# Opening of a fused transformer block on one core: where the first weight product's operands are loaded and cast, and in which order its last quarter and the first transposes run

## The chip, the cores and the metric

The kernel runs on one core of a Trainium2 chip. The metric is the device time of one execution in microseconds (us); the kernel before has a median of 939.83 us over three runs (939.63 to 941.84). The core has a matrix engine (TensorE, PE in the profile; its weight loads are listed apart as PEld), VectorE (DVE), ScalarE (ACT), GpSimd (POOL), and SyncE (SP), which in this kernel mostly issues transfers. Operands lie in SBUF, matrix results in PSUM; the inputs come by DMA.

## The reference, cut to what matters

Four blocks follow one another on a (2, 1024, 512) activation, each with a layer norm ahead of it and a residual around it:

```python
x = x + attn_a(layernorm(x), Wq, bq, Wk, bk, Wv, bv, Wbeta, ...)   # chunked linear attention, 4 heads of 128, chunks of 128
x = x + ffn(layernorm(x), wq_gate, s_gate, wq_up, s_up, wq_down, s_down)
x = x + attn_b(layernorm(x), W_q, W_k, W_v, W_o)                   # softmax attention over 1024 tokens, width 512
x = x + ffn(layernorm(x), ...)                                     # the same weights again

def layernorm(x): return (x - mean(x)) / sqrt(var(x) + 1e-5)

# attn_b
Q, K, V = x @ W_q, x @ W_k, x @ W_v
scores = (Q @ K.T) / sqrt(512)
out = softmax(scores) @ V @ W_o

# attn_a, its projections
q = x @ Wq + bq;  k = x @ Wk + bk;  v = x @ Wv + bv
```

Since `scores` is `x @ (W_q @ W_k.T) @ x.T`, the kernel computes the 512 x 512 matrix M = W_q W_k^T once, at the very beginning, and spills it for the third block. M does not depend on the activations, so it can run while the first activations are loaded and normalized. All large products are computed from pairs of numbers: a value is rounded to the matrix engine's fast 32-bit format (the high part), and what is lost is kept as a second number in the same format (the low part). A product of two such pairs is three matmuls: high x high, high x low, low x high.

## The kernel before, in words

Activations are worked on in tiles of 128 tokens x 512 features (16 tiles, NT), four tiles to a group. The code is written as a list of operations in program order; a planner decides from its own estimate of the times in which order each engine runs its own instructions, and adds the semaphores. Two helpers steer it: `behind(inss)` (line 61) makes every instruction that is written inside it come after the given instructions on the same engine's queue (it adds no wait across engines), and the tile pools fix how many buffers of a kind exist.

The opening, up to about 25 us:

- Line 347: `ones`, 128 x 128, filled by GpSimd. Lines 663 to 665: `WARM` = 8 matmuls of `ones` with `ones` in plain 32-bit format into a scratch bank (16 instructions in the trace, two to a matmul).
- `split` (line 68) is a cast by ScalarE into the high part and a subtraction for the low part, by VectorE unless another engine is given. `load_split` (line 73) is a transfer of 256 KB on SyncE's queue into a staging tile, and a `split` of it; the low part's instruction is kept in the list `parts`.
- `product_operands` (line 143) loads for each of four 128-row slices k of the contraction the left operand (W_q transposed) and the right operand (W_k transposed) with `load_split`. For M the low part of the right operand is computed by GpSimd (line 148). The first two slices use the four `stg` buffers, the last two a room that later takes Wq.
- Lines 676 to 680: the eight transfers for M, then four tiles of x, then the small gate weights. `split_M` is the last two low parts (the left one by VectorE, the right one by GpSimd).
- `weight_product` (line 152) is a generator. For each k it issues 12 matmuls (four output blocks of 128 rows, `mm3` each) and yields. Matmuls of one k can be ordered by the planner as it likes, except that each output bank accumulates.
- Lines 682 to 686: after k = 2 the tiles 0 and 1 are normalized and transposed by the matrix engine (four transposes a tile), the last slice k = 3 is put behind those transposes, and tiles 2 and 3 follow it.
- `layernorm` (line 100): statistics on VectorE (`bn_stats`, `bn_aggr`, `ve` = variance + eps), the power -1/2 on GpSimd (`rs`), then the normalized tile `xn` on VectorE. With `chained` a tile's `bn_stats` goes behind the `ve` of the tile before. `layernorm_T` (line 115) adds the four transposes and the split of their result into `xh` (ScalarE) and `xl` (VectorE).
- Line 687: Wk is loaded and split, its VectorE instructions behind the last `xn` and behind `split_M`. Then come the constants, Wq (staged in the room of M's operands), the first Wk product (`pWk`), the gate projection (`pab`, which reads `xh` and `xl` of all four tiles) and the Wq products (`pq`).

Of the kernel before, what the change touches and what calls it, by code (L numbers as in the profile page):

```python
# [9 lines left out]
F32 = mybir.dt.float32  # L10
# [3 lines left out]
ALU = mybir.AluOpType  # L14
AX = mybir.AxisListType

P = 128
D = 512
KD = D // P
# [8 lines left out]
NC = T // P  # L28
EPS = 1e-5
ZERO_POINT = 128.0  # L30
WARM = 8


@with_exitstack
def hybrid_block_kernel(ctx: ExitStack, tc: tile.TileContext, a, out):
    nc = tc.nc

    cp = ctx.enter_context(tc.tile_pool(name="const", bufs=1))
# [8 lines left out]
    def psum(name):  # L47
        return pp.tile([P, 512], F32, tag="ps", name=name)

    def slot(name, dt=F32R):  # L50

        return wp.tile([P, 2048], dt, tag="slot", name=name)


    ident = cp.tile([P, P], F32, name="ident")
    make_identity(nc, ident)
    mhalf = cp.tile([P, 1], F32, name="mhalf")
# [3 lines left out]
    def behind(inss):  # L61

        es = ExitStack()
        for ins in inss:
            es.enter_context(tc.issue_after(ins))
        return es

    def split(hi, lo, src, eng=None):

        c = nc.scalar.copy(hi, src)  # L70
        return c.ins, (eng or nc.vector).tensor_tensor(lo, src, hi.bitcast(F32), ALU.subtract).ins  # L71

    def load_split(w, sp, src_ap, name, eng=None, stg=None):

        if stg is None:
            stg = sp.tile([P, 512], F32, tag="stg", name=f"stg_{name}")
        load = nc.sync.dma_start(out=stg, in_=src_ap).ins
        cast, low = split(w[:, 0:512], w[:, 512:1024], stg, eng)
        parts.append(low)
        return cast, load  # L80


    def mm3(ps, lhs_hi, lhs_lo, rhs_hi, rhs_lo, first, last):
        nc.tensor.matmul(ps, lhs_hi, rhs_hi, start=first, stop=False)  # L84
        nc.tensor.matmul(ps, lhs_hi, rhs_lo, start=False, stop=False)  # L85
        end = nc.tensor.matmul(ps, lhs_lo, rhs_hi, start=False, stop=last).ins  # L86
        ends[id(ps)] = end
        return end

    ends, normed_x, parts, copied, varied = {}, [], [], [], []  # L90

    def new_xT(name):
        return tuple(slot(f"{n}_{name}").rearrange("p (k c) -> p k c", k=KD) for n in ("xh", "xl"))

    def load_x(src, name, tag="xin"):
        xin = (rp if tag == "xres" else xp).tile([P, D], F32, tag=tag, name=f"xin_{name}")
        nc.sync.dma_start(out=xin, in_=src)
        return xin

    def layernorm(xin, name, chained=False):  # L100

        bn = mp.tile([P, 6], F32, tag="bn", name=f"bn_{name}")
        with behind(varied if chained else ()):
            nc.vector.bn_stats(bn, xin)
        mv = mp.tile([P, 2], F32, tag="mv", name=f"mv_{name}")
        nc.vector.bn_aggr(mv, bn)
        ve = mp.tile([P, 1], F32, tag="ve", name=f"ve_{name}")
        varied[:] = [nc.vector.tensor_scalar(ve, mv[:, 1:2], EPS, None, ALU.add).ins]  # L108
        rs = mp.tile([P, 1], F32, tag="rs", name=f"rs_{name}")
        nc.gpsimd.tensor_tensor(rs, ve, mhalf, ALU.pow)  # L110
        xn = xp.tile([P, D], F32, tag="xn", name=f"xn_{name}")
        normed_x[:] = [nc.vector.tensor_scalar(xn, xin, mv[:, 0:1], rs, ALU.subtract, ALU.mult).ins]
        return xn

    def layernorm_T(xin, xT, i, name):

        xn = layernorm(xin, name, True)
        ps = psum(f"pxT_{name}").rearrange("p (k c) -> p k c", k=KD)
        for k in range(KD):
            turned = nc.tensor.transpose(ps[:, k, :], xn[:, k * P : (k + 1) * P], ident).ins  # L120
        xh, xl = xT
        cs = bass.ts(i, P)
        split(xh[:, :, cs], xl[:, :, cs], ps)
        return turned
# [18 lines left out]
    def product_operands(sp, lhsT_d, rhs_d, name, k, rooms=(None, None)):  # L143

        w = slot(f"{name}{k}")
        lw, rw = w[:, 0:1024], w[:, 1024:2048]
        load_split(lw, sp, lhsT_d[k * P : (k + 1) * P, :], f"{name}l{k}", None, rooms[0])
        eng = nc.gpsimd if name == "M" else None
        cast, _ = load_split(rw, sp, rhs_d[k * P : (k + 1) * P, :], f"{name}r{k}", eng, rooms[1])
        return lw, rw, cast  # L150

    def weight_product(operands, name):

        ps = [psum(f"p{name}{m}") for m in range(KD)]
        for k in range(KD):
            lw, rw, _ = operands[k]
            for m in range(KD):
                end = mm3(
                    ps[m],
                    lw[:, m * P : (m + 1) * P],  # L160
                    lw[:, 512 + m * P : 512 + (m + 1) * P],
                    rw[:, 0:512],
                    rw[:, 512:1024],
                    k == 0,
                    k == KD - 1,
                )
            yield ps, end

    def spill(pool, tags, ps, dst, name):
# [10 lines left out]
    def ln_norm(src, nm, st, i):  # L180


        t = st * ST + i
        for n in range(t, min(t + 2, st * ST + ST)):
            if (nm, n) not in lnX:
                lnX[nm, n] = load_x(src[n], f"{nm}{n}")
        if i == 0:
            lnY[nm, st] = yp.tile([P, 4, KD, ST, 32], F32, tag="y", name=f"y_{nm}{st}")
        xn = layernorm(lnX[nm, t], f"{nm}{t}")
        done = nc.vector.transpose(lnY[nm, st][:, :, :, i, :], xn.rearrange("p (k b q) -> p b k q", k=KD, b=4))  # L190
        laid[:] = [done.ins]
# [149 lines left out]
    with ExitStack() as actx:  # L341
        ap = actx.enter_context(tc.tile_pool(name="attn_a", bufs=2))
        a1 = actx.enter_context(tc.tile_pool(name="attn_a1", bufs=1))
        a3 = actx.enter_context(tc.tile_pool(name="attn_a3", bufs=3))
        sp = actx.enter_context(tc.tile_pool(name="stage", bufs=4))

        ones = a1.tile([P, P], F32, name="ones")
        nc.gpsimd.memset(ones, 1.0)

        le = a1.tile([P, P], F32, name="le")  # L350
        nc.gpsimd.affine_select(
            out=le, in_=ones, compare_op=ALU.is_ge, fill=0.0, base=0, pattern=[[1, P]], channel_multiplier=-1
# [11 lines left out]
        xTa, aba, gta, sca, qTa, kva, ata, deca, sta, rowa, facta = ({} for _ in range(11))  # L364
# [31 lines left out]
        xa = [x_in[t * P : (t + 1) * P, :] for t in range(NT)]  # L396

        def ln_tile(t):
            st, i = divmod(t, ST)
            if i == 0:  # L400
                xTa[st] = new_xT(f"a{st}")
            tag = "xres" if t < 8 and t % 4 > 1 else "xin"
            return layernorm_T(xs[t] if t < 4 else load_x(xa[t], f"a{t}", tag), xTa[st], i, f"a{t}")

        def gate_proj(st):

# [256 lines left out]
        pw = psum("warm")  # L663
        for i in range(WARM):
            nc.tensor.matmul(pw[:, 0:P], ones, ones, start=i == 0, stop=i == WARM - 1)
        loads, xs = [], []
        prep = weight_product(loads, "M")

        def staging(name):
# [5 lines left out]
        for k in range(KD):  # L675
            rooms = (room[:, 2 * k - 4], room[:, 2 * k - 3]) if k > 1 else (None, None)
            loads.append(product_operands(sp, a["WqT"], a["WkT"], "M", k, rooms))
        xs += [load_x(xa[t], f"a{t}", "xres" if t > 1 else "xin") for t in range(ST)]
        load_wab()
        split_M = parts[-2:]  # L680
        turned = []
        for k in range(KD):
            with behind(turned):
                pm, end = next(prep)
            with behind((end,)):
                turned = [ln_tile(t) for t in ((), (), (0, 1), (2, 3))[k]]
        with behind((*normed_x, *split_M)):
            load_wqkv("Wk")
        load_consts()
# [6 lines left out]
        for i in range(4):  # L696
            ends.clear()
            q_head(0, i)
            with behind((wq_loaded, *ends.values())):
                for t in ((), (4,), (5,), (6, 7))[i]:  # L700
                    ln_tile(t)
            if i == 1:
                with behind((*normed_x, *copied)):
                    spill(ap, ("kT", "kw", "sdec", "at"), pm, m_d, "M")
# [22 lines left out]
        for t in range(NT):  # L727
# [13 lines left out]
            if t == NT - 2:  # L741
                with behind(key_copy):
                    for n in (1, 2):
                        loads.append(product_operands(sp, a["WvT"], a["Wo"], "V", n))
                with behind(parts[-4:]):
                    late_norm.pop()()
# [28 lines left out]
            if t == NT - 2:  # L775
                prep = weight_product(loads, "V")
# [541 lines left out]
```

## Time and profile before

| what | value |
|---|---|
| median of three runs | 939.83 us (939.63 to 941.84) |
| the profiled execution, its own time | 939.53 us |
| its span, from the first to the last instruction | 937.8 us |
| TensorE busy | 931.0 us, 99% of the span |
| VectorE, ScalarE, GpSimd busy | 723.2, 411.1, 218.6 us |
| mean granted TensorE clock | 1.000 |
| first matmul of M starts | 4.93 us |
| first matmul of the first Wk product starts | 18.95 us |

In a line of the timeline the columns are: start in us from the first instruction, duration in us, engine, line of the code, operation, output and inputs by the program's names, sizes, and how many instructions were merged into the line; in brackets the idle time of the engine ahead of it and what ended that. For merged lines the duration is from the first start to the last end. In the table by stretch the columns are the length, and for each engine the busy time with the number of instructions, then the granted clock, the share of the time in which the DMA engines were busy, and their rate. `pM` is M in PSUM, `stg_Ml` and `stg_Mr` are the staged left and right operands of the first two slices, `y_M` those of the last two, `pxT_a` is a transposed tile.

### The profile page before, as it was taken

To read this page: it belongs to the slowest core of one execution; us is meant where nothing else is said; L and a number is where in the kernel's file an instruction comes from. 1 tells how busy PE (TensorE), PEld (TensorE's weight loads), DVE (VectorE), ACT (ScalarE), POOL (GpSimd) and SP (SyncE) were. 2 spreads that over 40 slices of the span, in tenths; PEclk is the share of its full clock that TensorE was granted. 3 is DMA by queue.
4 is the path that set the end of the run, shared out by engine and by line. 5 is a ranking of instruction groups with operands and counts; after the bars stand their busy time and mean duration, and the time that the engine had idled before them with its cause. 6 is when DMAs were issued, how large, how long until landed. Compare 5 with 4: busy or idle time off the path is not lost.

```text
span 937.8 us, 13217 instructions
## 1 busy us (share of the span) xinstructions
PE 931.0 (99%) x4402; PEld 773.1 (82%) x4402; DVE 723.2 (77%) x1461; ACT 411.1 (44%) x795; POOL 218.6 (23%) x320
## 2 busy tenths in 40 slices
PE   9999999999999999999999999999999999999998
PEld 7788888888778888888888888888878888888887
DVE  7867767779989799787947878658978876976655
ACT  5653434335665444444324535235434444434421
POOL 3233323444655001120120400031400531001100
PEclk9999999999999999999999999999999999999999
DMA  9536456585699566734852989326979852663012
GB/s 326 181 101 173 143 118 185 184 210 199 251 342 305 148 218 213 162 92 117 281 125 57 170 170 238 108 36 130 200 152 366 260 154 46 242 212 124 34 66 82
DMA packets 215605, 162.18 MB, mean 173 GB/s; under 512 B 150960, under 2 KB 166640, under 8 KB 215536
## 3 DMA queue, kind: packets, MB, share of 16 engines
q1 hardware_dynamic: 212624, 153.72, 56.4%
q0 software_dynamic: 2912, 7.61, 4.2%
q8 instruction: 35, 0.57, 0.3%
q14 instruction: 34, 0.28, 0.1%
HBM read 104.76 MB, written 41.84 MB: 156 GB/s over the span
## 4 chain that ended last, share of the span: by engine, by line
PE 94%; DMA 3%; DVE 1%; SPq 1%; issue 0%; ACT 0%; DVEq 0%; ACTq 0%
PE pog L901 4%; PE pog L900 4%; PE pof L901 4%; PE pof L900 4%; PE pVg L331 4%; PE pZg L331 4%; PE pXg L331 4%; PE pVf L331 4%; PE pZf L331 4%; PE pXf L331 4%; PE pob L86 3%; PE pob L84 3%; PE pob L85 3%; PE pYg L331 2%; PE pYf L331 2%; PE psV L1000 2%
## 5 line engine op out<-in xcount | busy, mean ns | idle before, releaser
L900 PE MATMUL pog<-wdg,hsg 128*128 128x512 f32 (+1 forms) x165 | 60.1, 375 | 0.0
L901 PE MATMUL pog<-wdg,hsg 128*128 128x512 f32 (+1 forms) x165 | 60.1, 375 | 0.0
L901 PE MATMUL pof<-wdf,hsf 128*128 128x512 f32 x154 | 59.2, 390 | 0.0
L900 PE MATMUL pof<-wdf,hsf 128*128 128x512 f32 x154 | 59.2, 389 | 0.0
L84 PE MATMUL pob<-vh,pth 128*128 128x512 f32 x128 | 50.1, 392 | 0.4 <-ACT pth L70 0.4
L86 PE MATMUL pob<-vh,ptl 128*128 128x512 f32 x128 | 50.2, 392 | 0.0
L85 PE MATMUL pob<-vl,pth 128*128 128x512 f32 x128 | 49.9, 390 | 0.0
L331 PE MATMUL pVf<-T_f,wcf 128*128 128x512 f32 x176 | 46.8, 390 | 0.0
L331 PE MATMUL pXg<-B_g,wcg 128*128 128x512 f32 x176 | 46.7, 389 | 0.0
L331 PE MATMUL pVg<-T_g,wcg 128*128 128x512 f32 x176 | 46.4, 389 | 0.0
L331 PE MATMUL pXf<-B_f,wcf 128*128 128x512 f32 x176 | 46.4, 392 | 0.0
L71 POOL TENSOR_TENSOR hsg<-sgg,hsg 128x128 fp32r<-128x128 f32 x40 | 18.0, 469 | 114.8 <-ACT hsg L70 78.8
L110 POOL TENSOR_TENSOR rs_g<-ve_g,mhalf 128x1 f32<-128x1 f32 x16 | 9.6, 604 | 134.3 <-DVE ve_g L108 134.3
L201 POOL DMA_DIRECT2D xT_g<-y_g x48 | 30.9, 651 | 40.6 <-DVE T_b L71 30.1
L331 PEld LDWEIGHTS pXf<-B_f,wcf 128*128 128x128 f32 x176 | 32.7, 188 | 7.7 <-issue 0.7
L110 POOL TENSOR_TENSOR rs_b<-ve_b,mhalf 128x1 f32<-128x1 f32 x16 | 10.4, 655 | 121.6 <-DVE ve_b L108 121.6
L331 PEld LDWEIGHTS pVf<-T_f,wcf 128*128 128x128 f32 x176 | 33.0, 188 | 7.0
L331 PEld LDWEIGHTS pXg<-B_g,wcg 128*128 128x128 f32 x176 | 33.1, 188 | 6.9
L331 PEld LDWEIGHTS pVg<-T_g,wcg 128*128 128x128 f32 x176 | 33.1, 188 | 6.9
L900 PEld LDWEIGHTS pog<-wdg,hsg 128*128 128x128 f32 x165 | 31.1, 188 | 5.7
L901 PEld LDWEIGHTS pog<-wdg,hsg 128*128 128x128 f32 x165 | 31.0, 188 | 5.6
L900 PEld LDWEIGHTS pof<-wdf,hsf 128*128 128x128 f32 x154 | 28.9, 188 | 6.0
(340 smaller groups left out, 2735.7 us busy)
## 6 DMA issues: line engine op xcount, KB each, us to landing
wcg<-wc SPq DMA_DIRECT2D x21, 896.0 KB, 5.2
wc<-wcf SPq DMA_DIRECT2D x11, 896.0 KB, 6.5
wcf<-wc SPq DMA_DIRECT2D x10, 896.0 KB, 6.6
p<-py SPq DMA_DIRECT2D x15, 512.0 KB, 3.9
ptl<-p SPq DMA_DIRECT2D x56, 128.0 KB, 3.9
xin_a<-in_x SPq DMA_DIRECT2D x16, 256.0 KB, 4.9
xra<-in_x SPq DMA_DIRECT2D x16, 256.0 KB, 3.0
row<-cl SPq DMA_DIRECT2D x16, 256.0 KB, 4.0
```

The costliest lines, as they stand in the source:

```text
L71: return c.ins, (eng or nc.vector).tensor_tensor(lo, src, hi.bitcast(F32), ALU.subtract).ins
L84: nc.tensor.matmul(ps, lhs_hi, rhs_hi, start=first, stop=False)
L85: nc.tensor.matmul(ps, lhs_hi, rhs_lo, start=False, stop=False)
L86: end = nc.tensor.matmul(ps, lhs_lo, rhs_hi, start=False, stop=last).ins
L110: nc.gpsimd.tensor_tensor(rs, ve, mhalf, ALU.pow)
L201: (nc.sync if sync else nc.gpsimd).dma_start(out=xf[32 * b : 32 * (b + 1), :, c, :], in_=y[32 * c : 32 * (c + 1), b].rearrange("p k i q -> ...
L331: nc.tensor.matmul(ps, w[:, m, k * P : (k + 1) * P], o[:, s, k, :], start=first and k == 0 and s == 0, stop=k == 1 and s == 1, skip_group_ ...
L900: nc.tensor.matmul(ps, hs[i][0][:, j], wd[j][:, ds], start=j == 0, stop=False)
L901: nc.tensor.matmul(ps, hs[i][1][:, j], wd[j][:, ds], start=False, stop=j == KH - 1)
L1000: ends[nm] = nc.tensor.matmul(ps, o[:, i, k], w[:, j, k], start=first and k == 0 and i + j == 0, stop=k == 1 and i == 1, skip_group_check= ...
```

## The change

Five edits, all in the opening:

1. `ones` is filled by VectorE, ahead of everything else in the program, and the warm-up has 6 matmuls in place of 8.
2. For M's first slice the right operand's transfer is issued on ScalarE's queue, the left one's on SyncE's as before. The right operand is cast by VectorE, the left one by ScalarE; the left low part is VectorE's, behind that cast; the right low part stays with GpSimd.
3. For the other three slices the low part of the right operand is computed by VectorE, and the casts and subtractions of M are put one behind the other in the order left, right, left, right.
4. The statistics of tiles 0 and 1 are issued on their own, behind M's last two low parts; `layernorm` takes them as known.
5. M's last slice is cut in two: output blocks 0 and 1 precede the transposes of tiles 0 and 1, blocks 2 and 3 follow them, then come tiles 2 and 3.

```diff
-WARM = 8
+WARM = 6
...
+    ones = cp.tile([P, P], F32, name="ones")
+    nc.vector.memset(ones, 1.0)
     ident = cp.tile([P, P], F32, name="ident")
...
-    def layernorm(xin, name, chained=False):
-
+    def statistics(xin, name, chained):
         bn = mp.tile([P, 6], F32, tag="bn", name=f"bn_{name}")
...
         nc.gpsimd.tensor_tensor(rs, ve, mhalf, ALU.pow)
+        return mv, rs
+
+    def layernorm(xin, name, chained=False, known=None):
+
+        mv, rs = known or statistics(xin, name, chained)
         xn = xp.tile([P, D], F32, tag="xn", name=f"xn_{name}")
...
-        load_split(lw, sp, lhsT_d[k * P : (k + 1) * P, :], f"{name}l{k}", None, rooms[0])
-        eng = nc.gpsimd if name == "M" else None
-        cast, _ = load_split(rw, sp, rhs_d[k * P : (k + 1) * P, :], f"{name}r{k}", eng, rooms[1])
+
+        first = name == "M" and k == 0
+        if first:
+            stg = [sp.tile([P, 512], F32, tag="stg", name=f"stg_M{n}0") for n in "lr"]
+            nc.scalar.dma_start(out=stg[1], in_=rhs_d[0:P, :])
+            nc.sync.dma_start(out=stg[0], in_=lhsT_d[0:P, :])
+            cast = nc.vector.tensor_copy(rw[:, 0:512], stg[1])
+            with behind((cast.ins,)):
+                casts[:] = split(lw[:, 0:512], lw[:, 512:1024], stg[0])
+            nc.gpsimd.tensor_tensor(rw[:, 512:1024], stg[1], rw[:, 0:512].bitcast(F32), ALU.subtract)
+            return lw, rw, cast.ins
+        queue_up = name == "M"
+        with behind((*parts[-1:], *casts) if queue_up else ()):
+            casts[:] = [load_split(lw, sp, lhsT_d[k * P : (k + 1) * P, :], f"{name}l{k}", None, rooms[0])[0]]
+        with behind((*parts[-1:], *casts) if queue_up else ()):
+            cast, _ = load_split(rw, sp, rhs_d[k * P : (k + 1) * P, :], f"{name}r{k}", None, rooms[1])
+            casts[:] = [cast]
         return lw, rw, cast
...
                     k == KD - 1,
                 )
+                if m == 1 and name == "M" and k == KD - 1:
+                    yield ps, end
             yield ps, end
...
-        ones = a1.tile([P, P], F32, name="ones")
-        nc.gpsimd.memset(ones, 1.0)
...
-        for k in range(KD):
+        known = {}
+        for k in range(KD + 1):
             with behind(turned):
                 pm, end = next(prep)
-            with behind((end,)):
-                turned = [ln_tile(t) for t in ((), (), (0, 1), (2, 3))[k]]
+            if k == 0:
+                with behind(split_M):
+                    for t in (0, 1):
+                        known[t] = statistics(xs[t], f"a{t}", True)
+            with behind((end, *varied)):
+                turned = [ln_tile(t) for t in ((), (), (), (0, 1), (2, 3))[k]]
```

## The prediction

> **What bounds the kernel now.** I read the engine totals first, then the waits of TensorE, then the opening in order of time, then the busy time by stretch. The totals:
>
> ```profile
> span 937.8 us, 13217 instructions
> ...
> PE 931.0 (99%) x4402; PEld 773.1 (82%) x4402; DVE 723.2 (77%) x1461; ACT 411.1 (44%) x795; POOL 218.6 (23%) x320
> ```
>
> TensorE is idle for 937.8 - 931.0 = 6.8 us in all. No edit shortens a product, so only idle time, the warm-up and slow spacing of matmuls can be won. TensorE's waits over the whole span:
>
> ```profile
> PE warm L665 <- POOL ones L348: 1.3, 1, 1.3
> PE pxT_a L120 <- DVE xn_a L112: 0.6, 1, 0.6
> PE pYf L331 <- DVE haf L828: 0.5, 1, 0.5
> PE pob L84 <- ACT pth L70: 0.4, 1, 0.4
> ```
>
> Two of the four lie in the opening, and the change aims at both. The opening in order of time:
>
> ```profile
> 1.27 3.78 PE L665 MATMUL warm<-ones 128*128 128x128 f32 x16 [1.27 <-POOL ones L348]
> ...
> 3.54 0.62 ACT L70 CAST M<-stg_Ml 128x512 fp32r<-128x512 f32 x1 [1.46 <-DMA stg_Ml<-in_WqT]
> ...
> 4.20 0.69 DVE L71 TENSOR_TENSOR M<-stg_Ml,M 128x512 fp32r<-128x512 f32 x1 [1.99 <-ACT M L70]
> 4.26 0.62 ACT L70 CAST M<-stg_Mr 128x512 fp32r<-128x512 f32 x1
> ...
> 4.93 1.38 PE L84 MATMUL pM<-M 128*128 128x512 f32 x4
> 4.96 1.29 POOL L71 TENSOR_TENSOR M<-stg_Mr,M 128x512 fp32r<-128x512 f32 x1 [3.16 <-ACT M L70]
> ...
> 6.30 0.50 PE L85 MATMUL pM<-M 128*128 128x512 f32 x1
> ...
> 8.10 2.94 DVE L71 TENSOR_TENSOR M<-y_M,M 128x512 fp32r<-128x512 f32 x2 [0.81 <-ACT M L70]
> ...
> 8.81 3.38 POOL L71 TENSOR_TENSOR M<-y_M,M 128x512 fp32r<-128x512 f32 x2
> ...
> 10.96 0.68 DVE L104 BATCH_NORM_STATS2 bn_a<-xin_a 128x6 f32<-128x512 f32 x1
> ...
> 14.89 0.66 PE L120 MATMUL pxT_a<-ident,xn_a 128*128 128x128 f32 x4 [0.60 <-DVE xn_a L112]
> ...
> 22.52 0.43 PE L411 MATMUL pab<-xl_a,wab 128*48 128x512 f32 x1
> ```
>
> Full-width matmuls follow each other by 0.227 us when nothing holds them (the four merged in 1.07 us at 8.25: three spacings and one length of 0.39). Against that, four losses are seen. The product begins at 4.93. Its first slice takes 8.25 - 4.93 = 3.32 us where 12 x 0.227 = 2.72 are needed: 0.60 lost, to slow first matmuls and to GpSimd's low part, which ends at 6.25 with L85 at 6.30. Tile 1's transposes start 0.87 after the last one of tile 0 where 0.11 is the step: 0.76 lost. And at 22.52 the gate projection starts 0.49 after the matmul before it: 0.26 lost, waiting for xl of tile 3 from VectorE. The table by stretch tells why the last matters:
>
> ```profile
> 11.00:18.90 7.90, 7.30 (x40) 5.98 (x39) 7.52 (x23) 3.70 (x9) 3.38 (x5) 1.00 1.05 356
> 18.90:25.00 6.10, 6.00 (x28) 4.19 (x27) 6.10 (x11) 3.69 (x8) 0.00 (x0) 1.00 1.05 390
> 25.00:41.70 16.70, 16.70 (x85) 13.47 (x85) 16.17 (x43) 12.20 (x23) 5.79 (x7) 1.00 0.64 217
> ```
>
> The third figure with a count in each line is VectorE: 7.52 of 7.90, then 6.10 of 6.10, then 16.17 of 16.70. From 11 to 41 us it has no room, so TensorE can't run ahead of it for long.
>
> **Part 1, warm-up.** `ones` comes from VectorE, whose first instruction now starts at 1.58; freed from waiting it can start about when GpSimd did its first (0.81) and needs a fill of about 0.20 (GpSimd's row), so the warm-up starts at about 1.1. Twelve passes in place of 16, 0.213 us each, take 3.78 - 4 x 0.213 = 2.93: it ends at 4.0, ahead of any operand. No gain by itself and no loss, if the matmuls after it run as fast as now; that is the second rival. What VectorE did at 1.58 to 2.2 (fold, gt) moves by 0.2 under its idle time up to 4.20.
>
> **Part 2, the first slice.** Now l0 lands at 3.52 and r0, issued 0.44 later on the same queue, at 4.24. Issued together, both land between 3.52 (no sharing) and 4.24 (all 512 KB by then, and l0 delayed). I take the middle, 3.9, since the DMA share was 0.78 of full in that time. ScalarE's issue (0.4, as SyncE's rows) fits ahead of its table load (0.81 to 2.09) and of the cast at 3.9. ScalarE's cast ends at 4.5. VectorE's cast of 512 columns is between 0.3 (half the next row) and 0.69 (two inputs); nearest is the xn row, one input, 0.55: 4.45. First matmul at 4.55, against 4.93.
>
> GpSimd's low part of r0 then starts at 4.5 beside VectorE's of l0. Alone they take 1.29 and 0.69; side by side the trace has 1.67 and 1.74 on GpSimd and 1.24 and 1.59 on VectorE (the pairs at 8.10 and 8.81). So r0's low part ends between 5.8 and 6.2; I take 5.9 and L85 at 5.95, against 6.30. The Trainium skill, page "SBUF — State Buffer", section "Who interferes with whom", has these two engines exclude each other for a whole instruction when both read SBUF so: VectorE would end at 4.5 + 1.29 + 0.69 = 6.5, the low x high matmuls would be late by up to 0.4, and the sum below would be 0.4 won in place of 0.5; the rows of 1.24 and 1.59, less than the 1.98 of such a sequence, speak for the smaller price. From L85 on the slice needs 1.87, so the second begins at 7.82 against 8.25: 0.43 won. Its right operand's cast ends at 7.42 as now, which covers it. SyncE issues everything behind r0 some 0.45 earlier, worth nothing: DMA is busy above 1.0 of its share from 5 us on.
>
> **Part 3, low parts.** Three GpSimd instructions go (1.29, 1.67, 1.74) and three come to VectorE. Between 6.6 and 11.0 VectorE has three low parts of 0.69, 1.24 and 1.59 = 3.52; alone, six take 6 x 0.69 = 4.14 at most (starts are 0.60 apart when queued, 3.6). Each waits for its cast; the last cast ends at 10.09, so the last low part ends at 10.8. The statistics start at 10.75 against 10.96: 0.2 won. Were the casts not in front, the three more would cost 3 x 0.60 = 1.8. Behind a low part that waits stand all later VectorE instructions, but until 10.8 these are only M's own.
>
> **Parts 4 and 5, half slice before the transposes.** Slices 2 and 3 start at 10.54 and 13.27; six matmuls end at 14.63. Both statistics in a row take 2 x 1.0, powers 0.57 beside them: xn of tile 0 by 13.5, of tile 1 by 14.3 (now 13.31 and 14.84). Eight transposes then run without the 0.76: to 15.6. Second half 1.45, to 17.05; eight transposes 0.9, to 17.95 against 18.95: 1.0 won for TensorE if xn of tile 3 is there by 17.4. It ends at 18.25 now; with VectorE 0.2 ahead and its list unchanged, 18.05; with the two xl, which now come later than it, moved behind it (2 x 0.6), 16.9.
>
> **The sum.** TensorE is 1.0 ahead at 18. VectorE, with the same work and no idle time, is 0.2 ahead, so xl of tile 3 is there at 22.26 and the gate projection can start at 22.3. That is the next thing late. Bounds: 0.2 won (order unchanged) to 1.0 (the planner takes the xl ahead of Wq's low parts, which have some 2 us to spare: the last ends at 24.27, its matmul comes near 26.9). The stretch with VectorE at 6.10 of 6.10 is nearest to the low end: I take 0.5. Behind 42 us nothing is touched, and TensorE's order carries the gain to the end. Profiled time 939.53 - 0.5 = 939.03; the median shown lies 0.30 above the profiled run, so 939.83 - 0.5 = **939.3 us**.
>
> **Rivals.** (a) TensorE's lead holds: the planner fills the wait with the high-part matmuls of pq and pab (0.23 each, at least six are ready) and moves the xl. For it: the two Wq low parts in front of them are not urgent. Against: no free VectorE time before 41 us. All of 1.0, and up to the 0.26: 938.7.
>
> (b) Slower: the fast clock comes later. The granted clock reads 1.00 throughout, yet the 128-wide passes are 0.213 apart in the warm-up, while the eight of pd at 51.44 take 0.89, about 0.112 each; and the first product's spacing falls from 0.52 to 0.23 within 0.5 us of 4.93, some 3.7 to 4.2 us after the warm-up began. A shorter warm-up leaves 4.0 to 4.55 empty. If that restarts the count, speed comes at about 8.5: nine matmuls at 0.43 (0.227 x 0.213/0.112), three at 0.23, second slice at 9.1: 0.9 late. Parts 4 and 5 give back 0.76 at most, VectorE's cap then costs nothing: between +0.1 and +0.9, I take 0.5: 940.3. It decides if the first slice ends later than 8.25. The Trainium skill, page "TensorE: Matmul & The Clock Gate", section "Part 1: The HAM clock gate", says that the clock follows a free-running window of about 3.4 us and not a number of matmuls; by it a hole of 0.5 us costs nothing or a whole window, by chance.
>
> (c) The change does nothing: both transfers land at 4.24, the contention takes the rest, VectorE's start is unmoved: 939.8.
>
> (d) The planner reorders later stages. Their largest waits now are 0.65, 0.58 and 0.32 us, so a few new ones give +/-1.5; above 2.8 it takes many.
>
> **How the numbers follow.** About 0.3% (2.8 us) is what a measurement of this kernel can tell from no change. Everything the opening loses, 0.77 (a start at 4.16, l0's cast end) + 0.60 + 0.76 + 0.26 = 2.4, is less. Forecast 0.42, (a) 0.22, (b) 0.14, (c) 0.10, (d) 0.12. Faster by over 0.3% 0.04, slower 0.07, both from (d) mainly. The range reaches from (a) with its whole 1.3 and a little of (d), 938.0, to (b) at its end, 940.9.
>
> **What would show it.** Right: first L84 at 4.4 to 4.7; L85 under 6.2; M's low parts on VectorE at 0.69; statistics near 10.75; no gap in the transposes; pWk at 18.0 to 18.7; a wait of pab on xl larger than 0.26. Wrong: spacing of 0.43 in the first slices; pWk later than 18.95; new waits behind 42 us.

## The result, and the profile after

The changed kernel takes 942.50 us (median of twelve runs, 940.47 to 943.71); the kernel before took 939.73 us in the twelve runs beside it. The ratio is 1.0027, with an interval from 1.0018 to 1.0035: the change costs some 2.5 us where 0.5 us were to be won, and the time lies 1.6 us above the top of the range, 940.9. The profiled execution took 943.01 us.

The totals of the changed kernel's page:

```profile
span 941.3 us, 13211 instructions
...
PE 932.0 (99%) x4398; PEld 773.3 (82%) x4398; DVE 724.3 (77%) x1466; ACT 410.1 (44%) x794; POOL 215.2 (23%) x316
```

TensorE's idle time rose from 6.8 to 941.3 - 932.0 = 9.3 us, its busy time by 1.0 us although it has four matmuls less: some of them ran slower. What it waited for, the four longest first (total, times, longest):

```profile
PE pM L86 <- ACT M L72: 1.8, 1, 1.8
PE warm L687 <- DVE ones L56: 1.1, 1, 1.1
PE pXf L353 <- DVE hbf L858: 0.7, 1, 0.7
PE pXf L353 <- DMA wcf<-wc: 0.6, 1, 0.6
```

The 0.6 for the transposes is gone from this list, the warm-up starts 0.14 earlier (1.13 against 1.27), and at the top stands a new wait of 1.84 us: the first matmul of M for its left operand's cast. The opening in order of time:

```profile
0.81 0.41 ACTq L157 DMA_DIRECT2D stg_Mr<-in_WkT  x1
0.81 0.39 SPq L79 DMA_DIRECT2D y_M<-in_WqT  x1
...
1.13 2.93 PE L687 MATMUL warm<-ones 128*128 128x128 f32 x12 [1.13 <-DVE ones L56]
...
1.25 0.42 SPq L158 DMA_DIRECT2D stg_Ml<-in_WqT  x1
...
4.68 0.43 DVE L159 CAST M<-stg_Mr 128x512 fp32r<-128x512 f32 x1 [2.61 <-DMA stg_Mr<-in_WkT]
...
5.19 1.27 POOL L162 TENSOR_TENSOR M<-stg_Mr,M 128x512 fp32r<-128x512 f32 x1 [3.52 <-DVE M L159]
...
5.23 1.30 ACT L72 CAST M<-stg_Ml 128x512 fp32r<-128x512 f32 x2 [2.70 <-DMA stg_Ml<-in_WqT]
...
5.90 2.08 PE L86 MATMUL pM<-M 128*128 128x512 f32 x4 [1.84 <-ACT M L72]
...
7.78 1.91 PE L87 MATMUL pM<-M 128*128 128x512 f32 x4
...
9.48 1.36 PE L88 MATMUL pM<-M 128*128 128x512 f32 x4
...
10.54 0.68 DVE L105 BATCH_NORM_STATS2 bn_a<-xin_a 128x6 f32<-128x512 f32 x1
...
10.68 1.07 PE L86 MATMUL pM<-M 128*128 128x512 f32 x4
...
17.49 1.03 PE L126 MATMUL pxT_a<-ident,xn_a 128*128 128x128 f32 x8
...
18.20 1.00 DVE L118 TENSOR_SCALAR xn_a<-xin_a,mv_a,rs_a 128x512 f32<-128x512 f32 x2 [2.71 <-PE pxT_a L126]
...
20.54 0.48 PE L86 MATMUL pWk<-Wk,xh_a 128*128 128x512 f32 x1
...
24.66 0.43 PE L433 MATMUL pab<-xl_a,wab 128*48 128x512 f32 x1 [0.34 <-DVE xl_a L73]
```

Three things are to be seen. First, SyncE's first transfer (0.81) is not M's left operand but the left operand of a later slice (`y_M`); the one that the first matmul needs is second, at 1.25. It lands at 5.21, ScalarE starts at 5.23, TensorE at 5.90. Second, the matmuls from 5.90 follow each other by (7.78 - 5.90) / 4 = 0.47 and then by (9.48 - 7.78) / 4 = 0.43 us; only at 10.1 does the step fall to 0.23. Third, VectorE stands idle for 2.71 us before 18.20, waiting for TensorE's transposes.

The chain of time against the kernel before, stage by stage (starts of the named matmuls in the two traces; the last row is the first matmul of `pcum`, near 40 us):

| from, to | before | after | difference |
|---|---|---|---|
| start to first matmul of M | 4.93 | 5.90 | +0.97 |
| to the second slice | 3.32 | 4.78 | +1.46 |
| to the first Wk product | 10.70 | 9.86 | -0.84 |
| to the gate projection's first `xl` matmul | 3.57 | 4.12 | +0.55 |
| to `pcum` | 17.69 | 17.59 | -0.10 |
| sum | 40.21 | 42.25 | +2.04 |

Behind that every engine has the instructions of the kernel before in the same order. The two spans still differ there by 895.04 - 893.60 = 1.44 us, counted to the start of TensorE's last matmul; that stretch ran from 892.8 to 896.6 over the fourteen traces of this study, also between kernels that differ only in the warm-up. In the changed kernel 1.24 us of it are the two waits at `pXf` in the list above; whether they belong to the change is taken up with the open ends.

### The profile page after: what moved, and what is told of

It reads as the page before. It is cut to its first block, busy times and chain, and to the rows that moved or that the text cites. A ratio compares the mean times of both kernels' runs of the same rounds, so it can differ in the third digit from the quotient of the medians.

```text
span 941.3 us, 13211 instructions
## 1 busy us (share of the span) xinstructions
PE 932.0 (99%) x4398; PEld 773.3 (82%) x4398; DVE 724.3 (77%) x1466; ACT 410.1 (44%) x794; POOL 215.2 (23%) x316
## 4 chain that ended last, share of the span: by engine, by line
PE 92%; DMA 4%; DVE 2%; ACT 1%; SPq 1%; issue 0%; DVEq 0%; ACTq 0%
PE pog L928 4%; PE pog L927 4%; PE pof L928 4%; PE pof L927 4%; PE pVg L353 4%; PE pZg L353 4%; PE pXg L353 4%; PE pXf L353 4%; PE pVf L353 4%; PE pZf L353 4%; PE pob L88 2%; PE pob L86 2%; PE pob L87 2%; PE pYg L353 2%; PE pYf L353 2%; PE psV L1027 2%
```

## The experiments

Two theories stood after the trace. **Order**: the loss is the transfer that SyncE issues first; put right, the forecast's gain appears. **Clock**: the loss is the slow spacing, which comes of the warm-up that ends at 4.06 with a hole (TensorE without work) behind it. In the expectations, Theory A is the clock and Theory B the order; C, D and E are explained where they stand.

**The left operand first.** Two lines of part 2 change places, nothing else:

```diff
-            nc.scalar.dma_start(out=stg[1], in_=rhs_d[0:P, :])
             nc.sync.dma_start(out=stg[0], in_=lhsT_d[0:P, :])
+            nc.scalar.dma_start(out=stg[1], in_=rhs_d[0:P, :])
```

> The changed kernel with the two transfers of the first slice written in the other order, so that the left operand is the first on SyncE's queue again. Theory A (the hole in TensorE's work between warm-up and product makes the slow spacing begin anew, and the late left operand makes the hole): both operands land near 4.5 to 4.7, first matmul near 5.2 in place of 5.90, still 0.43 apart until some 4 us later, second slice at 9.9 in place of 10.68, total 0.7 us less than the changed kernel. Theory B (the late left operand alone costs the time, the slow spacing has nothing to do with the hole): full spacing from the start, second slice near 8.2, total 2.0 us or more below the changed kernel, level with the kernel before or faster.

Measured: 941.31 against 940.36 us, 1.0008 (1.0000 to 1.0017). The opening of this kernel:

```profile
1.12 2.93 PE L687 MATMUL warm<-ones 128*128 128x128 f32 x12 [1.12 <-DVE ones L56]
...
4.96 1.17 PE L86 MATMUL pM<-M 128*128 128x512 f32 x4 [0.91 <-ACT M L72]
...
6.75 0.50 PE L87 MATMUL pM<-M 128*128 128x512 f32 x1 [0.62 <-POOL M L162]
```

The left operand now lands at 4.19 and the first matmul is at 4.96, 0.94 sooner than in the changed kernel. So the order of two lines decides which transfer SyncE issues first. Yet 4.96 is no earlier than the 4.93 of before. In this execution the matmuls ran at the full step in spite of a hole of 0.91, and then stood 0.62 for GpSimd's low part of the right operand. The profiled execution was the fastest of twelve (939.15, and the slowest 942.45), so the median is not read from it. By the two ratios the time fell by some 1.8 us, near the 2.0 of Theory B, but the second slice came at 8.70 and not near 8.2, and one trace does not speak for the other eleven executions.

**The warm-up lengthened up to the product.** In the changed kernel:

```diff
-WARM = 6
+WARM = 12
```

> The changed kernel with 12 warm-up matmuls in place of 6. Theory A: 24 passes from 1.13, 0.213 apart until about 5.2 and 0.112 after, end near 5.8, so no hole; first matmul at 5.90 as in the changed kernel but 0.227 apart, second slice at 8.7 in place of 10.68, total 1.5 to 2.0 us below the changed kernel (about 940.7). Theory C (VectorE's queue, with three more low parts and the statistics, sets the time at 24 us whatever the first slice does): second slice earlier, but the gate projection still near 24.6 and the total as in the changed kernel (942.5).

Measured: 941.94 us, 1.0012 (1.0004 to 1.0021).

```profile
1.12 5.00 PE L687 MATMUL warm<-ones 128*128 128x128 f32 x24 [1.12 <-DVE ones L56]
5.97 1.20 PE L86 MATMUL pM<-M 128*128 128x512 f32 x4
...
8.82 1.07 PE L86 MATMUL pM<-M 128*128 128x512 f32 x4
...
23.99 0.43 PE L433 MATMUL pab<-xl_a,wab 128*48 128x512 f32 x1 [1.29 <-DVE xl_a L73]
```

The first matmul is as late as in the changed kernel (5.97), but the first slice takes 2.85 us instead of 4.78: without the hole the slow spacing is gone. Of the 1.9 us only 0.67 arrive at the gate projection (23.99 against 24.66), because the planner now put xl of tile 3 behind one low part of Wq and one statistics instruction more; a new wait of 1.29 us took over.

**Both put right.** The changed kernel with the two lines exchanged, and

```diff
-WARM = 6
+WARM = 8
```

> The changed kernel with the left operand first on SyncE's queue and 8 warm-up matmuls, so that the warm-up ends near 4.9, where the product starts; every edit but the shorter warm-up is in it, without its hole. Theory A: TensorE is at full spacing by the first or second matmul in every run; first matmul near 4.95, one wait of up to 0.8 for GpSimd's low part, second slice at 8.2 to 8.7, gate projection at 22.2 to 22.8, total level with the kernel before (within 0.5 us) and 2 us below the changed kernel. Theory D (ScalarE's queue, not the order on SyncE's, costs the time): the second slice is later than 8.7 and the total stays over 1 us above the kernel before.

Measured: 939.89 against 940.51 us, 0.9995 (0.9986 to 1.0003). With both undone the loss is gone.

```profile
1.12 3.78 PE L687 MATMUL warm<-ones 128*128 128x128 f32 x16 [1.12 <-DVE ones L56]
4.83 1.41 PE L86 MATMUL pM<-M 128*128 128x512 f32 x4
...
6.61 0.49 PE L87 MATMUL pM<-M 128*128 128x512 f32 x1 [0.37 <-POOL M L162]
```

Each of the two mended alone leaves some 0.8 to 1.1 us above the kernel before, neither mended 2.5, both none: the loss has two parts, and the interval of this kernel lies wholly below that of the changed one. The parts are not cut cleanly, since the exchanged lines also shorten the hole, from 1.84 to 0.91 us.

**The warm-up alone.** The kernel before with part 1 only:

```diff
-WARM = 8
+WARM = 6
...
+    ones = cp.tile([P, P], F32, name="ones")
+    nc.vector.memset(ones, 1.0)
...
-        ones = a1.tile([P, P], F32, name="ones")
-        nc.gpsimd.memset(ones, 1.0)
```

> The kernel before with the first edit alone (ones by VectorE, 6 warm-up matmuls). Warm-up ends at 4.06, first matmul at 4.93, a hole of 0.87. Theory A in its strict form (any hole starts the count anew): the first slice is 0.43 apart, second slice at 9.4 to 9.9 in place of 8.25, total 1.0 to 1.5 us above the kernel before. Theory A in its weak form (only a hole of the length of the changed kernel's 1.84 does): first slice as before, total unchanged within 0.3 us.

Measured: 941.66 us, 1.0009 (0.9999 to 1.0018).

```profile
4.88 2.08 PE L86 MATMUL pM<-M 128*128 128x512 f32 x4 [0.83 <-ACT M L72]
...
8.46 0.57 PE L87 MATMUL pM<-M 128*128 128x512 f32 x1
8.88 0.39 PE L88 MATMUL pM<-M 128*128 128x512 f32 x1
```

With all else as before, a hole of 0.83 us is enough: the steps are 0.43 until about 8.9, and the second slice starts at 9.57 instead of 8.25. At the first Wk product 0.50 of these 1.32 us is left (19.45 against 18.95), at the gate projection 0.23 (22.75 against 22.52). So the opening alone does not account for the ratio of 1.0009, whose interval just takes in no change.

**The same two again**, for how fixed the slow spell is: the changed kernel and part 1 alone, one more trace of each.

> The changed kernel once more, for its trace. Theory A with the clock's own beat (the fast clock comes at the end of a stretch of fixed length that was busy enough, and where these stretches lie is chance): product at 5.8 to 6.0, and the slow spacing of 0.43 ends at another time than 10.2, between 8.6 and 12, or is not there at all (about one run in four). If the count begins with the product's first matmul: it ends 4.2 to 4.4 us after that again. Waits of 0.7 to 0.85 us near 394 and 401 us are chance: they need not come again.

> The kernel before with the first edit alone, once more, for its trace. By the clock's own beat the slow spacing ends at another time than 8.4, anywhere from 4.9 (none seen) to 8.4. If the count begins with the product's first matmul: it ends 3.5 us after that, at 8.4, again.

Measured: 944.23 and 941.58 us, one execution each. TensorE in the changed kernel's second trace:

```profile
6.11 2.07 PE L86 MATMUL pM<-M 128*128 128x512 f32 x4 [2.05 <-ACT M L72]
...
9.69 1.91 PE L88 MATMUL pM<-M 128*128 128x512 f32 x4
11.39 0.81 PE L86 MATMUL pM<-M 128*128 128x512 f32 x2
```

This time the step stayed at 0.43 through the whole first slice, to about 11.8; the second slice came at 11.39. Part 1 alone was slow until about 9.1. So for one kernel the end of the slow spell moves by 0.3 to 1.7 us between executions.

**The clock in all fourteen traces.** The tables by stretch read 1.00 throughout only because they take a stretch without a clock record for full speed. The trace's own record of the full clock begins later, at the very moments when the step falls to 0.23. Its first entry lasts 931.84 or, in three traces, 935.25 us. The difference is 3.41, and the two are 273 and 274 times that. So here the clock is granted on a beat of 3.41 us, and where the beat lies against the program differs from one execution to the next. The table gives TensorE's busy time in the beat that ends with the grant and in those ahead of it:

| trace | full clock from | busy of 3.41 us ahead of it | in the beats before |
|---|---|---|---|
| changed kernel | 10.06 | 3.41 | 1.58, before that 2.10 |
| changed kernel again | 11.80 | 3.41 | 2.28, before that 2.49 |
| part 1 alone | 8.84 | 3.41 | 2.58 |
| part 1 alone again | 9.11 | 3.41 | 2.62 |
| left operand first | 3.99 | 2.87 | 0 |
| buffers for `xn`, below | 4.35 | 2.93 | 0 |
| the eight without a hole | 4.48 to 6.08 | 3.21 to 3.41 | up to 1.40 |

In every trace the full clock comes with the end of the first beat in which TensorE was busy for 2.87 us or more, and never after one with 2.62 or less. A warm-up of 2.93 us fills such a beat only where the beat lies almost exactly over it; where the beat takes in the hole, one or two more beats pass at the slow step. By these bounds an estimate is that one execution in six to one in three escapes.

**Parts 3 to 5 alone.** The changed kernel without parts 1 and 2: `WARM = 8`, `ones` by GpSimd, and no branch for the first slice.

```diff
-        first = name == "M" and k == 0
-        if first:
-            ...
-            return lw, rw, cast.ins
```

> The kernel before with all right low parts of M by VectorE, the early statistics and the cut last slice; loading, casts and warm-up as before. Theory A: nothing of these costs time; the 0.76 at the transposes goes, VectorE's end sets the rest, total 0.3 to 0.8 us below the kernel before (939.0 to 939.4). Theory C: VectorE's three more low parts push its whole list, the gate projection starts later than 22.5, total above the kernel before by up to 1.8 us.

Measured: 939.72 against 940.36 us, 0.9989 (0.9981 to 0.9998).

```profile
1.27 3.57 PE L677 MATMUL warm<-ones 128*128 128x128 f32 x16 [1.27 <-POOL ones L358]
4.94 1.19 PE L84 MATMUL pM<-M 128*128 128x512 f32 x4
...
7.80 1.07 PE L84 MATMUL pM<-M 128*128 128x512 f32 x4
...
14.61 1.03 PE L124 MATMUL pxT_a<-ident,xn_a 128*128 128x128 f32 x8
...
17.71 0.47 PE L84 MATMUL pWk<-Wk,xh_a 128*128 128x512 f32 x1
...
22.10 0.44 PE L423 MATMUL pab<-xl_a,wab 128*48 128x512 f32 x1 [0.35 <-DVE xl_a L71]
```

The eight transposes of tiles 0 and 1 run as one group, and the Wk product starts at 17.71 against 18.95, 1.24 sooner. At the gate projection 0.42 of it is left (22.10 against 22.52), and TensorE waits there for VectorE's xl: the cap that the forecast named. The time came out as the recorded Theory A had it. The repeat of the same kernel:

> The fifth experiment once more (low parts, statistics and cut slice on the kernel before), since the tenth, which differs by two buffers, came out level. If these edits win what the prediction gave them (0.2 to 1.0 us): 939.5 to 940.3 beside 940.5 for the kernel before, gate projection at 22.1, or up to 1.4 later when the third and fourth transfers land late, as in the tenth. If the fifth was luck: level or slower, gate projection no earlier than 22.5.

Measured: 940.33 against 940.73 us, 0.9998 (0.9987 to 1.0008), so one interval excludes no change and the other doesn't. Its Wk product started at 18.24, its gate projection at 22.63, 0.11 later than before.

**The same with `ones` by VectorE**, which is the kernel with both put right less part 2:

```diff
+    ones = cp.tile([P, P], F32, name="ones")
+    nc.vector.memset(ones, 1.0)
...
-        ones = a1.tile([P, P], F32, name="ones")
-        nc.gpsimd.memset(ones, 1.0)
```

> As the run before it, but the first slice loaded and cast as in the kernel before (both transfers on SyncE's queue, both casts by ScalarE, the right low part by VectorE): the two runs differ in the second edit alone. Theory A: landings 3.5 and 4.2, first matmul 4.9, second slice at 7.8, gate projection at 22.0, total 0.5 to 1.2 us below the kernel before; the second edit by itself then costs 0.3 to 0.9 us of time in place of winning 0.4. If the second edit wins what was forecast of it, the run before this one is the faster of the two.

Measured: 940.17 against 940.51 us, 0.9995 (0.9986 to 1.0003), to the fourth digit what the version with two queues gave (part 2's other edits included). In the traces the single queue is ahead: second slice 7.71 against 8.56, gate projection 21.78 against 22.64. The 0.3 to 0.9 us that part 2 was expected to cost were not seen in the time either. Part 2, with its second queue, wins nothing.

**Buffers for xn.** VectorE's idle 2.71 us in the changed kernel ended with the transposes: `xn` has two buffers, so tile 2's waits until tile 0's is read. Tiles 2 and 3 get buffers of their own, in the changed kernel and in parts 3 to 5 alone:

```diff
+    xn_rooms = {}
...
-        xn = xp.tile([P, D], F32, tag="xn", name=f"xn_{name}")
+        own = xn_rooms.pop(name, None)
+        xn = own or xp.tile([P, D], F32, tag="xn", name=f"xn_{name}")
...
+        xn_rooms.update({n: a1.tile([P, D], F32, name=f"xn_{n}") for n in ("a2", "a3")})
```

> The changed kernel with own buffers for the normalized tiles 2 and 3, so that they need not wait for the transposes of tiles 0 and 1 to free theirs. Theory E (a price that the prediction missed: with two buffers, TensorE's lateness stops VectorE for 2.7 us and so reaches the gate projection whole): xn of tile 2 at 15.5 in place of 18.2, VectorE's list up to xl of tile 3 ends 0.5 to 1.0 us earlier for the same first slice, total 0.4 to 1.0 us below the changed kernel. Rival (VectorE then waits at xl of tile 0, which needs the same transposes, and the time is TensorE's anyway): no change of the total beyond 0.3 us.

> Low parts, statistics and cut slice on the kernel before (as in the fifth experiment), with the same two more buffers. Without a late TensorE the buffers are free nearly in time (xn of tile 2 at 15.64 there): at most 0.3 us won over that run, 0.5 to 1.2 us below the kernel before.

Measured: 941.67 against 940.48 us, 1.0008 (0.9999 to 1.0018) on the changed kernel, and 940.64 against 940.48 us, 1.0000 (0.9989 to 1.0011) on parts 3 to 5, where 0.5 to 1.2 us below the kernel before were expected. The first's trace:

```profile
5.98 1.20 PE L86 MATMUL pM<-M 128*128 128x512 f32 x4 [1.93 <-ACT M L72]
...
8.84 1.07 PE L86 MATMUL pM<-M 128*128 128x512 f32 x4
...
15.54 0.55 DVE L120 TENSOR_SCALAR xn_a<-xin_a,mv_a,rs_a 128x512 f32<-128x512 f32 x1
...
16.89 0.69 DVE L73 TENSOR_TENSOR xl_a<-pxT_a,xh_a 128x512 fp32r<-128x512 f32 x1 [0.53 <-ACT xh_a L72]
```

The wait for the transposes is gone (tile 2's xn at 15.54), a wait of 0.53 for the transposes' cast takes its place one instruction later. The time fell by some 1.7 us against the changed kernel, and the intervals only touch, at 1.0018; but this trace has the full step from the first slice on, with the same warm-up and a hole of 1.93 us (its beat ended at 4.35), and was the fastest of its eleven runs (938.99, the slowest 943.15). How much of the 1.7 us is the buffers' stays open. Compared with the trace of the long warm-up, which had two buffers and the full step, Wk's low parts end at 21.05 against 20.95: with TensorE on time the buffers move nothing, and with parts 3 to 5, where TensorE is on time, they won nothing.

**Relieving VectorE.** Parts 3 to 5 with these buffers, and two of Wq's low parts given to GpSimd:

```diff
-                w, eng = wqkv[nm][k], nc.gpsimd if k % 2 and nm == "Wv" else None
+                w, eng = wqkv[nm][k], nc.gpsimd if (k % 2 and nm == "Wv") or (k < 2 and nm == "Wq") else None
```

> As the run before it, with the low parts of the first two slices of Wq by GpSimd, which is idle from 17 to 27 us, so that one VectorE instruction less stands ahead of xl of tile 3. If VectorE's queue holds the gate projection (the step of the prediction that limits the gain): xl of tile 3 ends 0.4 to 0.6 us earlier, gate projection near 21.5 in place of 22.1, total 0.3 to 0.6 us below the run before it and 0.8 to 1.6 us below the kernel before. If the two engines' shared reading eats it (GpSimd beside VectorE made a VectorE low part 1.24 to 1.59 in place of 0.69): no gain.

Measured: 941.32 against 940.48 us, 1.0009 (1.0001 to 1.0018).

```profile
18.78 3.59 DVE L71 TENSOR_TENSOR Wk<-stg_Wk,Wk 128x512 fp32r<-128x512 f32 x4
...
20.28 3.23 POOL L71 TENSOR_TENSOR Wq<-y_Wq,Wq 128x512 fp32r<-128x512 f32 x2 [2.60 <-DMA y_Wq<-in_Wq]
```

Wk's four low parts took 3.59 us beside GpSimd instead of 2.49 alone. VectorE loses 1.10 on them and is spared two of 0.60, so the gate projection is not earlier (23.62 against 23.48 in the run without this edit).

## Why the prediction was wrong, step by step

- **Part 2, the transfers: the first step that failed.** "Issued together, both land between 3.52 and 4.24" took for granted that the left operand stays first on SyncE's queue. ScalarE's issue is written ahead of SyncE's, and the planner gave the first place to another transfer: 5.21 instead of 3.9, the first matmul at 5.90 instead of 4.55. Exchanging the lines showed the cause. Even then "the middle" was too good: 4.05 to 4.19 and 4.23 to 4.36 with two queues, against 3.52 and 4.24 with one. The left operand pays 0.5 to 0.7 for sharing, and the right one isn't there sooner.
- **Part 1, "no gain and no loss if the matmuls run as fast as now": the second.** The condition failed, as rival (b) described: a step of 0.43 behind the hole. (b) had 0.14 of the chance and at most +0.9 us, because it let the full step return at about 8.5. Part 1 alone was slow until 8.8 and 9.1, the changed kernel until 10.1 and 11.8: right in kind, short in size. Its point of decision held: the first slice ended at 10.68, past 8.25.
- **The other rivals.** Nothing was planned anew behind the opening, against (d); TensorE's lead did not hold, against (a); and of (c) it came true that the second queue wins nothing, though only with the lines exchanged did both operands land near its 4.24.
- **The clock's rule.** The prediction read 1.00 in the table by stretch as the granted clock, where the trace has no record, and let a hole restart a count. By the fourteen traces it is no count from the first matmul but a beat of 3.41 us. In the kernel before, the warm-up reached the product, so no beat held a hole; the change's six matmuls end 0.8 us or more ahead of it. Which executions escape is chance. The Trainium skill, page "TensorE: Matmul & The Clock Gate", section "Part 1: The HAM clock gate", has a free-running window of about 3.4 us decide; the traces agree, with 3.41. The prediction cited this, with a hole that costs "nothing or a whole window, by chance", which is what came, and still priced it as a mishap of +0.5.
- **Part 2, the low part by GpSimd.** Forecast to end at 5.9, it ended at 6.46 in the changed kernel, where it ran alone but started only at 5.19, and at 6.69 and 6.55 with the lines exchanged, where it ran beside VectorE. The prediction read 1.24 and 1.59 us of before as a smaller price than a full sequence. In the traces one of the two engines ends a fixed time after the other, as if it began only then. With the lines exchanged:

```profile
4.87 0.69 DVE L73 TENSOR_TENSOR M<-stg_Ml,M 128x512 fp32r<-128x512 f32 x1
4.90 1.79 POOL L162 TENSOR_TENSOR M<-stg_Mr,M 128x512 fp32r<-128x512 f32 x1 [3.23 <-DVE M L159]
...
5.73 1.51 DVE L73 TENSOR_TENSOR M<-stg_Ml,M 128x512 fp32r<-128x512 f32 x1 [0.17 <-ACT M L72]
```

  VectorE ends at 5.56, GpSimd 1.13 later at 6.69, and VectorE's next 0.55 later at 7.24. The rows of before fit too: GpSimd's second low part ended at 7.50 + 1.29 = 8.79, and VectorE's 1.24 from 8.10 ended 0.55 after that. So the Trainium skill, page "SBUF — State Buffer", section "Who interferes with whom", whose price was set aside, was the better guide, with the engines in the other order than the prediction's sum by it had them.
- **Part 3: right.** Low parts follow each other by 0.60 on VectorE, and the statistics start at 10.54 (forecast 10.75).
- **Parts 4 and 5: right for TensorE.** No gap in the transposes; second slice to Wk product in 9.86 instead of 10.70 us, 0.84 won where 0.76 was the term. Alone, pWk started at 17.71 and 18.24, in or just ahead of the forecast 17.95 to 18.7.
- **The sum's cap: right without parts 1 and 2.** VectorE's xl holds the gate projection, and 1.24 us at 18 became 0.42 at 22. Three measurements of these parts gave 0.9989, 0.9995 and 0.9998, about 0.6 us faster on average, near the 0.5 forecast, and a fourth, with the two more buffers, 1.0000. So the gain is not shown beyond doubt.
- **What no step had:** TensorE's lateness passes to VectorE through the two `xn` buffers. The forecast spoke of VectorE having "no idle time"; it had 2.71 us of it, once TensorE was late. That is seen in the trace; its share of the loss was not isolated.

Still open: two waits of TensorE far behind the opening. In the changed kernel:

```profile
394.01 1.17 PE L353 MATMUL pXf<-B_f,wcf 128*128 128x512 f32 x4 [0.69 <-DVE hbf L858]
...
401.19 1.16 PE L353 MATMUL pXf<-B_f,wcf 128*128 128x512 f32 x4 [0.55 <-DMA wcf<-wc]
```

Both stand in all four traces with the slow spell, for 1.2 to 1.6 us together, and in none of the ten others (two of these have one wait of 0.3 and 0.8 us near 398). In the same four, the eight `xT_b` transfers that SyncE issues ahead of the weights wanted there take 9.6 to 9.9 us to issue, in the ten 6.9 to 7.8. So 1.24 of the 3.5 us by which the changed kernel's trace is longer may come with the slow spell, although they lie near 400 us. How the one leads to the other, or whether something else leads to both, no run shows; the order of the instructions there is the same.

No version tried is clearly faster than the kernel before.

## What to carry to other kernels

Before a transfer is moved to another queue, work out which transfer the old queue will issue first, and ask whether the two share the bandwidth anyway. A warm-up must last until the first real matmul has its operands: it is measured by its end, not by its count. Behind 2.93 us of warm-up, holes of 0.8 to 2.1 us left nine to thirteen matmuls at half speed in four traces and none in two. Work taken from one vector engine to relieve another is priced by a pair that runs together, and a lead won on TensorE is followed to the next engine that has no idle time before it is counted.

## What the runs showed of the hardware that was not expected

- The step of full-width matmuls was 0.43 or 0.23 us while the table by stretch read 1.00; the trace's record of the full clock begins where the step changes, for one kernel at 10.06 in one execution and at 11.80 in another, on a beat of 3.41 us. Plain 128-wide passes of the warm-up were 0.21 apart and, in the warm-up of 24 passes, 0.11 from about 5.5 us on.
- Two-input subtractions on 128x512 by VectorE and GpSimd side by side: the later one ends 0.55 (VectorE) or 1.13 to 1.15 us (GpSimd) after the other's end.
- The third and fourth transfers of 256 KB, issued alike on the one queue, landed between 5.2 and 7.2 and between 6.3 and 7.8 us. In parts 3 to 5 with more buffers the late ones (7.18, 7.83) put the second slice at 8.53 instead of 7.80: chance of the size of the effect that was sought.
